# A long convolution ahead of adapters and a gated FFN: order of the first loads, smaller kernel groups, other engines for part of the elementwise work, TensorE in source order

## The chip, the cores and the metric

The kernel runs on one core of one Trainium2 chip, in float32. The metric is device microseconds of one execution, the median of three runs. Engine names are those of the profile: PE is TensorE (PEld its weight load), DVE VectorE, ACT ScalarE, POOL GpSimd, SP SyncE. ACTq and SPq are the instruction streams of ACT and SP where they issue DMAs.

## The reference

x has 32 sequences of 64 channels and 1024 steps. Four residual stages follow each other; the change concerns the first.

```python
# 0: S4D convolution along the 1024 steps, one kernel per channel h
dt = exp(log_dt); A = -exp(log_A_real) + 1j * A_imag; dtA = A * dt[:, None]
Ct = (C[..., 0] + 1j * C[..., 1]) * (exp(dtA) - 1.0) / A
K = 2.0 * einsum('hn,hnl->hl', Ct, exp(dtA[:, :, None] * arange(1024))).real   # 64 states n
y = irfft(rfft(x, n=2048) * rfft(K, n=2048))[..., :1024] + x * D[:, None]
x = x + y * (arange(1024) < length[:, None, None])
# 1, 2: a 1024x1024 weight per sequence, chosen by an index
x = x + einsum('bsi,boi->bso', x, weight1[ids1])
x = x + einsum('bij,bkj->bik', x, weight2[ids2])
# 3: gated FFN, 2752 hidden units, low-rank adapters of rank 16 by index
x = x + ffn(x)
```

## The kernel before

**Stages.** x is held transposed in four chunks of eight sequences (`xs[c]`, 2 MB each): positions within a block of 128 on the partitions; block, sequence and channel along the free side. `convolution` (from L533) does stage 0 for all chunks. Chunks 2 and 3 are then parked in DRAM. `adapters(0)` does stages 1 and 2 of chunk 0, and `ffn(c)` does stage 3 of chunk c with the adapters of chunk c + 1 woven in between. Adapter weights (`wa`, 512 KB a load, 512 loads) go through a pool of nine buffers.

**The order of work.** A scheduler places each instruction in its engine's stream by the order of the source and by when it expects the operands; each engine then runs its own stream strictly in that order and waits on semaphores. Tiles of a tag share a number of buffers, and a tile waits for its buffer to come free. `tc.manual_schedule(engines={PE})` takes TensorE's stream out of the scheduler's hands: its instructions run in the order of the source. Before, it covers only what follows the convolution (L525). `tc.issue_after(ins)` puts what it encloses behind `ins` in the same engine's stream, with no wait for `ins` to end.

**The first loads.** SP issues the constant table `cst` (L105), the ids (L110, L114), the state space parameters `par` (L552), the lengths `ln` (L554), and then the first three `uf`. ACT issues the four loads of x (L668) at the same time. From `par` VectorE works out exp, sine and cosine of small tiles (128x64), the discretised coefficients (L584 to L655) and the mask of the lengths (L662).

**The convolution kernels, `kernels(g)`.** A group is 16 heads (channels), four groups. The kernel of a head is 1024 numbers, written as 32x32: position l = 32a + b, so exp(dtA l) is a product of two factors. `powers` (L690) makes angles `theta` (`bth`) and logarithms of sizes `rho` (`brho`) for both factors by multiplying a column per head with a table along l: four VectorE multiplications of 128x512. `rho` goes through Exp on ACT; three sines (`sine`, L570: seven VectorE instructions each and one Sin on ACT), and five more products on VectorE give `gt` and `et`. TensorE multiplies them, a 32x32 product a head (`pk`, L721). VectorE copies the result out (`ks`, L729) and adds D in the first position (L731). ACT's queue stores it to DRAM in rows (`kp`, L734) behind a row of zeros (L733). The tiles of `kernels` have one buffer per tag, `gt`, `et`, `ks` two.

**The convolution proper, `convolve(g, kp)`.** For four heads at a time, `uf` (x of these heads in reversed order, 512 KB, L741) is loaded, and for each pair of heads `hk` (1 MB, L746): the Toeplitz matrix, read from `kp` with a step of one element from partition to partition. Both have three buffers. Eight matmuls of falling width a head accumulate into `pc` (L757), VectorE multiplies with the mask into `tmp` (two buffers, L764), and four VectorE additions, one for each chunk, add `tmp` to x (L775). The loop of L777 to L781 traces `kernels(g + 1)` before `convolve(g)`.

Of the kernel before, what the change touches and what calls it, by code (L numbers as in the profile page):

```python
# [32 lines left out]
NE = 16  # L33
NPIECE = 2 * BC
AT_GATED, AT_DOWN = 4, 5
HG = 16
LQ = 32
KROW = P + L

# [22 lines left out]
def kernel(  # L62
# [39 lines left out]
        return psum.tile([P, 512], F32, tag="acc", name=name, bufs=2)  # L102

    cst = cpool.tile([P, CO_N], F32, tag="cst", name="cst")
    nc.sync.dma_start(cst, consts)  # L105
    ident = cst[:, CO_ID : CO_ID + P]
    bmask = cst[:, CO_BM : CO_BM + TC]

    ids_sb = cpool.tile([1, 3 * B], I32, tag="ids", name="ids_sb")
    nc.sync.dma_start(ids_sb, ids)  # L110
# [9 lines left out]
    for c in range(NCK):  # L120
# [4 lines left out]
            None,  # L125
            ALU.add,
        )

    def x_tile(pool, c, tag):
        return pool.tile([P, KT, TC], F32, tag=tag, name=f"x{c}")

    xs = [x_tile(xpool, c, "x") for c in range(2)]
    parked = []
    with tc.tile_pool(name="x2pool", bufs=1) as x2pool:
        late = [x_tile(x2pool, c, f"x{c}") for c in range(2, NCK)]
        convolution(tc, cst, xt, xf, ssm, lens, xs + late, ps_tile)
        for c, x_c in enumerate(late, 2):
            d = dpool.tile([P, KT, TC], F32, tag=f"xd{c}", name=f"xd{c}")  # L140
            nc.scalar.dma_start(d, x_c)
            parked.append(d)

# [248 lines left out]
    def prepare(c):  # L392

        x_c = xs[c]
        for name, table in (("g", ag), ("u", au)):
            at = columns(table, c, KT, f"{name}_{c}")
            low_rank(at, KT, lambda i: (x_c[:, i, :], P), tms[name], f"{name}_{c}")
        xq = [
            x_c[:, k * KH : (k + 1) * KH, t * TH : (t + 1) * TH]
            for k in (0, 1)  # L400
            for t in (0, 1)
        ]

        xd = hpool.tile([P, 7, KH, TH], F32, tag="xd", name=f"xd_{c}")
        for i, q in enumerate((0, 2, 3)):
            nc.scalar.copy(xd[:, 4 + i], xq[q])
        xb = moving(*xq, *(xd[:, i] for i in range(4)))
        return (xd[:, 4], xd[:, 5], xd[:, 6], *xb[3:])
# [113 lines left out]
                    other(AT_DOWN)  # L522
        return ready

    with tc.manual_schedule(engines={PE}):  # L525
        for _ in adapters(0):
            pass
        xb = prepare(0)
        for c in range(NCK):
            xb = ffn(c, xb, adapters(c + 1) if c + 1 < NCK else iter(()))  # L530


def convolution(tc, cst, xt, xf, ssm, lens, xs, ps_tile):  # L533

# [8 lines left out]
    with ExitStack() as ctx:  # L543
# [6 lines left out]

        par = s1.tile([P, 6, H], F32, tag="par", name="par")
        nc.sync.dma_start(par, ssm)  # L552
        ln = s1.tile([P, B], I32, tag="len", name="ln")
        nc.sync.dma_start(ln, lens.partition_broadcast(P))  # L554
        aim, cre, cim, dskip = (par[:, i, :] for i in range(2, 6))
# [108 lines left out]
            )  # L664
        maskf = mask.rearrange("p k b -> p (k b)")

        for c in range(NCK):
            nc.scalar.dma_start(xs[c], xt[:, c])  # L668

        zero = s1.tile([HG, P], F32, tag="zero", name="zero")  # L670
        nc.vector.memset(zero, 0.0)

        def kernels(g):

            h0 = g * HG
            shape = [P, HG, LQ]

            def over_l(ap):
                return ap[:, h0 : h0 + HG].unsqueeze(2).to_broadcast(shape)

            def over_h(at):
                return cst[:, at : at + LQ].unsqueeze(1).to_broadcast(shape)

            n = [0]

            def big(tag):
                n[0] += 1
                return s1.tile(shape, F32, tag=f"b{tag}", name=f"b{tag}{g}_{n[0]}")

            def powers(at, tag):  # L690
                theta, rho = big(f"th{tag}"), big(f"rho{tag}")
                tt(theta, over_l(y), over_h(at), ALU.mult)
                tt(rho, over_l(x), over_h(at), ALU.mult)
                nc.scalar.activation(rho, rho, AF.Exp)
                return theta, rho

            th1, rho1 = powers(CO_LVAL, "1")
            th2, rho2 = powers(CO_LVAL + LQ, "2")

            def flat_sine(theta, i, tag):  # L700
# [10 lines left out]
            gt = s2.tile(shape, F32, tag="gt", name=f"gt{g}")  # L711
            et = s2.tile(shape, F32, tag="et", name=f"et{g}")
# [7 lines left out]
            for i in range(HG):  # L720
                nc.tensor.matmul(  # L721
                    ps[:LQ, i * LQ : (i + 1) * LQ],
                    gt[:, i, :],
                    et[:, i, :],
                    start=True,
                    stop=True,
                )
            ks = s2.tile([LQ, HG, LQ], F32, tag="ks", name=f"ks{g}")
            nc.vector.tensor_copy(ks.rearrange("a h b -> a (h b)"), ps[:LQ, : HG * LQ])  # L729
            k0 = ks[0:1, :, 0]  # L730
            tt(k0, k0, dskip[0:1, h0 : h0 + HG], ALU.add)  # L731
            kp = dram.tile([HG, KROW], F32, tag=f"kp{g}", name=f"kp{g}")
            nc.scalar.dma_start(kp[:, :P], zero)  # L733
            nc.scalar.dma_start(kp[:, P:].rearrange("h (a b) -> a h b", b=LQ), ks)  # L734
            return kp

        def convolve(g, kp):
            for h0 in range(0, HG, 4):
                ha = g * HG + h0
                uf = s3.tile([P, 4, KT, B], F32, tag="uf", name=f"uf{ha}")  # L740
                nc.sync.dma_start(uf, xf[:, ha : ha + 4])  # L741
                tmp = s2.tile([P, 4, KT * B], F32, tag="tmp", name=f"tmp{ha}")
                for i in range(0, 4, 2):
                    hk = s3.tile([P, 2, L], F32, tag="hk", name=f"hk{ha + i}")

                    nc.sync.dma_start(  # L746
                        hk,
                        bass.AP(
                            tensor=kp.tensor,
                            offset=kp[h0 + i : h0 + i + 1, 1:2].offset,  # L750
                            ap=[[1, P], [KROW, 2], [1, L]],
                        ),
                    )
                    ps = ps_tile(f"pc{ha + i}").rearrange("p (i t) -> p i t", i=2)
                    for j in range(2):
                        for d in range(KT):
                            nc.tensor.matmul(  # L757
                                ps[:, j, d * B :],
                                hk[:, j, d * P : (d + 1) * P],
                                uf[:, i + j, : KT - d, :].rearrange("p k b -> p (k b)"),  # L760
                                start=(d == 0),
                                stop=(d == KT - 1),
                            )
                    tt(  # L764
                        tmp[:, i : i + 2, :],
                        ps,
                        maskf.unsqueeze(1).to_broadcast([P, 2, KT * B]),
                        ALU.mult,
                    )
                tv = tmp.rearrange("p i (k b) -> p k b i", b=B)  # L770
                for c in range(NCK):
                    xv = xs[c].rearrange("p k (b h) -> p k b h", h=H)[
                        :, :, :, ha : ha + 4
                    ]
                    tt(xv, xv, tv[:, :, c * BC : (c + 1) * BC, :], ALU.add)  # L775

        ready = kernels(0)  # L777
        for g in range(H // HG):
            nxt = kernels(g + 1) if g + 1 < H // HG else None
            convolve(g, ready)  # L780
            ready = nxt  # L781


# [131 lines left out]
```

## Time and profile before

| what | value |
|---|---|
| time, median of 3 runs | 2580.82 us (2580.62 to 2581.64) |
| the profiled execution: time | 2580.24 us |
| the profiled execution: span | 2578.5 us |
| PE busy | 2483.8 us (96%) |
| DVE busy | 1061.7 us (41%) |
| ACT busy | 255.5 us (10%) |
| POOL busy | 45.8 us (2%) |
| first pk on PE | 40.4 us after the span's start |
| first pc on PE | 61.5 us |
| last mask multiplication (tmp) | 212.7 us |
| first adapter matmul (pa) | 214.1 us |

The span runs from the first to the last instruction of the profiled execution; the time counts what lies around it too. "Busy" counts an instruction's duration; idle time in the profile is put down to what ended it, the releaser. The chain of waits follows the work that ended last back through releasers; a stretch of it that belongs to PE cannot be shortened by another engine.

### The profile page before, as it was taken

The numbers are of one execution on the slowest core, as the hardware profiler recorded it, in microseconds if no ns is written. First come the engines' busy times: TensorE is split into PE (matmuls) and PEld (weight loads), VectorE is DVE, ScalarE is ACT, GpSimd is POOL, SyncE is SP. The second block draws the span as 40 slices with busy tenths as digits, with TensorE's granted clock in tenths as the row PEclk, the third lists the DMA queues.
The fourth block names the chain that finished last, engine by engine and source line by source line (L and its number), as shares of the span: only waits on it lengthen the run. The fifth ranks groups of instructions, "written<-read, shape, count | busy, mean of one in ns | idle before, by whom it ended". The sixth has DMA issues, their size and how long they took to land.

```text
span 2578.5 us, 33259 instructions
## 1 busy us (share of the span) xinstructions
PE 2483.8 (96%) x12896; PEld 1795.9 (70%) x12896; DVE 1061.7 (41%) x2174; ACT 255.5 (10%) x468; POOL 45.8 (2%) x52
## 2 busy tenths in 40 slices
PE   1998999999999999999999999999999999999999
PEld 0994225767676686667776686667766688888877
DVE  8632004343334353333334453343334354444444
ACT  3100001010001101110011100110010101100110
POOL 0000000000000000000000000000000000000000
PEclk9999999999999999999999999999999999999999
DMA  7787997464746447554746547555655443223212
GB/s 288 258 281 271 406 409 270 172 230 152 241 156 231 168 151 263 182 213 155 244 163 226 171 137 265 189 203 171 217 197 207 163 145 107 84 70 108 82 52 67
DMA packets 176160, 500.63 MB, mean 194 GB/s; under 512 B 19778, under 2 KB 69122, under 8 KB 174978
## 3 DMA queue, kind: packets, MB, share of 16 engines
q1 hardware_dynamic: 145762, 453.63, 50.0%
q10 hardware_dynamic: 26144, 31.24, 3.5%
q0 software_dynamic: 4096, 13.63, 1.8%
q8 instruction: 102, 1.67, 0.3%
q14 instruction: 56, 0.46, 0.1%
HBM read 485.56 MB, written 12.88 MB: 193 GB/s over the span
## 4 chain that ended last, share of the span: by engine, by line
PE 90%; DMA 7%; DVE 2%; ACT 0%; ACTq 0%; issue 0%; SPq 0%; DVEq 0%
PE pf L351 42%; PE po L480 21%; PE pa L182 14%; PE pc L757 6%; DMA wa<-in_w 5%; PE pf L298 4%; PE py L200 1%; PE pl_d L275 1%; PE po L298 1%; DMA x<-xd 1%; DMA out_y<-x 0%; DMA ln<-in_lens 0%; PE pl_g L275 0%; PE pl_u L275 0%; DMA raw_g<-in_ag 0%
## 5 line engine op out<-in xcount | busy, mean ns | idle before, releaser
L351 PE MATMUL pf<-xd,wf 128*128 128x256 f32 (+1 forms) x2816 | 677.9, 384 | 0.0
L351 PEld LDWEIGHTS pf<-xd,wf 128*128 128x128 f32 (+1 forms) x2816 | 517.8, 187 | 131.4 <-issue 58.8
L182 PE MATMUL pa<-wa,x 128*64 128x512 f32 x2048 | 494.1, 602 | 25.6 <-DMA wa<-in_w 20.6
L351 PE MATMUL pf<-xd,s 128*128 128x256 f32 (+1 forms) x2112 | 507.9, 383 | 2.2 <-DVE s L319 2.2
L351 PEld LDWEIGHTS pf<-xd,s 128*128 128x128 f32 (+1 forms) x2112 | 388.8, 187 | 86.7 <-issue 31.9
L182 PEld LDWEIGHTS pa<-wa,x 128*64 128x64 f32 x2048 | 149.3, 137 | 335.1 <-issue 250.4
L480 PE MATMUL po<-act,wd 128*128 128x256 f32 x704 | 177.0, 385 | 0.0
L480 PE MATMUL po<-actd,wd 128*128 128x256 f32 x704 | 172.9, 379 | 0.0
L480 PE MATMUL po<-actd,s 128*128 128x256 f32 x704 | 172.9, 379 | 0.0
L376 DVE TENSOR_TENSOR c<-pf,c 128x256 f32<-128x256 f32 (+1 forms) x88 | 37.3, 424 | 328.8 <-PE pf L351 328.8
L480 PEld LDWEIGHTS po<-act,wd 128*128 128x128 f32 x704 | 130.3, 190 | 33.3 <-issue 11.0
L757 PE MATMUL pc<-uf,hk 128*128 128x256 f32 (+7 forms) x1024 | 149.1, 309 | 0.0
L757 PEld LDWEIGHTS pc<-uf,hk 128*128 128x128 f32 x1024 | 145.2, 192 | 3.6
L480 PEld LDWEIGHTS po<-actd,s 128*128 128x128 f32 x704 | 133.6, 190 | 18.4
L480 PEld LDWEIGHTS po<-actd,wd 128*128 128x128 f32 x704 | 133.6, 190 | 18.4
L318 DVE TENSOR_TENSOR s<-wf 128x512 f32<-128x512 f32 x88 | 60.7, 689 | 143.3 <-DMA wf<-in_wu 65.9
L379 DVE TENSOR_TENSOR c<-pf,u 128x256 f32<-128x256 f32 (+1 forms) x88 | 37.3, 424 | 169.5 <-PE pf L298 169.5
L204 DVE TENSOR_TENSOR x<-py,x 128x512 f32<-128x512 f32 x64 | 41.3, 686 | 153.0 <-PE py L200 152.7
L381 DVE TENSOR_TENSOR c<-pf,u 128x256 f32<-128x256 f32 (+1 forms) x88 | 37.3, 424 | 132.4 <-PE pf L351 132.4
L318 DVE TENSOR_TENSOR s<-wd 128x384 f32<-128x384 f32 x64 | 33.4, 521 | 141.2 <-PE po L480 81.4
L192 ACT COPY y<-pa 128x512 f32<-128x512 f32 x64 | 37.5, 586 | 499.7 <-PE pa L182 475.1
L480 PE MATMUL po<-act,s 128*128 128x256 f32 (+1 forms) x352 | 86.5, 379 | 0.0
(147 smaller groups left out, 1574.0 us busy)
## 6 DMA issues: line engine op xcount, KB each, us to landing
wa<-in_w SPq DMA_DIRECT2D x512, 512.0 KB, 6.7
wf<-in_wg SPq DMA_DIRECT2D x88, 512.0 KB, 3.6
wf<-in_wu SPq DMA_DIRECT2D x88, 512.0 KB, 3.6
wd<-in_wd SPq DMA_DIRECT2D x96, 384.0 KB, 4.0
hk<-kp SPq DMA_DIRECT2D x32, 1024.0 KB, 7.4
x<-in_xt ACTq DMA_DIRECT2D x4, 2048.0 KB, 11.4
uf<-in_xf SPq DMA_DIRECT2D x16, 512.0 KB, 8.5
wd<-in_wd SPq DMA_DIRECT2D x32, 256.0 KB, 3.7
```

Source lines behind the costliest of these rows:

```text
L182: nc.tensor.matmul(acc[i][s * H : (s + 1) * H, :], xs[c][:, kt, lo + s * H : lo + (s + 1) * H], wts[s][:, i * 512 : (i + 1) * 512], start= ...
L192: nc.scalar.copy(y[:, i * 512 : (i + 1) * 512], acc[i])
L200: nc.tensor.transpose(ps[:, i, :], y[:, (q + i) * P : (q + i + 1) * P], ident)
L204: nc.vector.tensor_add(cols, ps, cols)
L298: nc.tensor.matmul(ps, b[rows_], t[rows_], start=start, stop=True, skip_group_check=True,)
L318: nc.vector.tensor_add(s1, a21, a22)
L351: nc.tensor.matmul(ps, ws[j][:, kt, :n], xb[j][:, kt, :], start=start and kt == 0, stop=kt == KH - 1, skip_group_check=True,)
L376: nc.vector.tensor_add(cq[:n, 3], pb, cq[:n, 3])
L379: nc.vector.tensor_add(cq[:n, 2], pc, u[:n])
L381: nc.vector.tensor_add(cq[:n, 1], pb, u[:n])
L480: nc.tensor.matmul(pss[j], ws[j][:k, i, :], ab[m - m0][j], start=(m == m0 and home[j] % 2 == 0), stop=(m == m1 - 1), skip_group_check=True,)
L757: nc.tensor.matmul(ps[:, j, d * B :], hk[:, j, d * P : (d + 1) * P], uf[:, i + j, : KT - d, :].rearrange("p k b -> p (k b)"), start=(d == ...
```

## The change

- `consts` is loaded inside `convolution`, after `par`; the loads of the ids and the four index instructions made from them are traced after the convolution.
- The four loads of x move from ahead of the groups to behind the store of the first group's kernels in ACT's stream.
- The groups are 8, 8, 12, 12, 12 and 12 heads instead of four of 16; tiles keep the size of the largest and are cut.
- The four multiplications of `powers` and the four additions to x go to GpSimd. ACT copies `pk` out instead of VectorE.
- `convolve` now does four heads; `kernels(g + 1)` is traced between the last but one and the last four heads of group g.
- `manual_schedule` covers the whole kernel, so TensorE's stream in the convolution is in the order of the source too.

```diff
-HG = 16
+GROUPS = (8, 8, 12, 12, 12, 12)
+HG = max(GROUPS)
...
     cst = cpool.tile([P, CO_N], F32, tag="cst", name="cst")
-    nc.sync.dma_start(cst, consts)
...
+    ctx.enter_context(tc.manual_schedule(engines={PE}))
+    with tc.tile_pool(name="x2pool", bufs=1) as x2pool:
+        late = [x_tile(x2pool, c, f"x{c}") for c in range(2, NCK)]
+        convolution(tc, cst, consts, xt, xf, ssm, lens, xs + late, ps_tile)
...
     ids_sb = cpool.tile([1, 3 * B], I32, tag="ids", name="ids_sb")
     nc.sync.dma_start(ids_sb, ids)
...
-    with tc.tile_pool(name="x2pool", bufs=1) as x2pool:
-        late = [x_tile(x2pool, c, f"x{c}") for c in range(2, NCK)]
-        convolution(tc, cst, xt, xf, ssm, lens, xs + late, ps_tile)
...
         nc.sync.dma_start(par, ssm)
+        nc.sync.dma_start(cst, consts)
         ln = s1.tile([P, B], I32, tag="len", name="ln")
...
-        for c in range(NCK):
-            nc.scalar.dma_start(xs[c], xt[:, c])
...
+        loaded = []
         def kernels(g):
-            h0 = g * HG
-            shape = [P, HG, LQ]
+            h0, hg = sum(GROUPS[:g]), GROUPS[g]
+            shape = [P, hg, LQ]
...
-                tt(theta, over_l(y), over_h(at), ALU.mult)
-                tt(rho, over_l(x), over_h(at), ALU.mult)
+                nc.gpsimd.tensor_tensor(theta, over_l(y), over_h(at), ALU.mult)
+                nc.gpsimd.tensor_tensor(rho, over_l(x), over_h(at), ALU.mult)
...
-            nc.vector.tensor_copy(ks.rearrange("a h b -> a (h b)"), ps[:LQ, : HG * LQ])
+            ks = s2.tile([LQ, HG, LQ], F32, tag="ks", name=f"ks{g}")[:, :hg]
+            nc.scalar.copy(ks.rearrange("a h b -> a (h b)"), ps[:LQ, : hg * LQ])
...
-            nc.scalar.dma_start(kp[:, :P], zero)
-            nc.scalar.dma_start(kp[:, P:].rearrange("h (a b) -> a h b", b=LQ), ks)
+            nc.scalar.dma_start(kp[:, :P], zero[:hg])
+            load = nc.scalar.dma_start(kp[:, P:].rearrange("h (a b) -> a h b", b=LQ), ks)
+            loaded.append(load.ins)
...
-        def convolve(g, kp):
-            for h0 in range(0, HG, 4):
+        def convolve(kp, row, ha):
...
-                    tt(xv, xv, tv[:, :, c * BC : (c + 1) * BC, :], ALU.add)
+                nc.gpsimd.tensor_tensor(xv, xv, tv[:, :, c * BC : (c + 1) * BC, :], ALU.add)
         ready = kernels(0)
-        for g in range(H // HG):
-            nxt = kernels(g + 1) if g + 1 < H // HG else None
-            convolve(g, ready)
+        for c in range(NCK):
+            with tc.issue_after(loaded[0]):
+                nc.scalar.dma_start(xs[c], xt[:, c])
+        ha = 0
+        for g, hg in enumerate(GROUPS):
+            nxt = None
+            for row in range(0, hg, 4):
+                convolve(ready, row, ha)
+                ha += 4
+                if row + 8 == hg and g + 1 < len(GROUPS):
+                    nxt = kernels(g + 1)
             ready = nxt
```

More of the change, by code (lines that the diff above doesn't have):

```diff
@@ L104, with x_tile @@
     cst = cpool.tile([P, CO_N], F32, tag="cst", name="cst")
-    nc.sync.dma_start(cst, consts)
     ident = cst[:, CO_ID : CO_ID + P]
     bmask = cst[:, CO_BM : CO_BM + TC]
+    def x_tile(pool, c, tag):
+        return pool.tile([P, KT, TC], F32, tag=tag, name=f"x{c}")
+    xs = [x_tile(xpool, c, "x") for c in range(2)]
+    parked = []
+    ctx.enter_context(tc.manual_schedule(engines={PE}))
+    with tc.tile_pool(name="x2pool", bufs=1) as x2pool:
+        late = [x_tile(x2pool, c, f"x{c}") for c in range(2, NCK)]
+        convolution(tc, cst, consts, xt, xf, ssm, lens, xs + late, ps_tile)
+        for c, x_c in enumerate(late, 2):
+            d = dpool.tile([P, KT, TC], F32, tag=f"xd{c}", name=f"xd{c}")
+            nc.scalar.dma_start(d, x_c)
+            parked.append(d)
     ids_sb = cpool.tile([1, 3 * B], I32, tag="ids", name="ids_sb")
@@ L127 @@
         )
[L131 to L135, printed above, removed]
-    with tc.tile_pool(name="x2pool", bufs=1) as x2pool:
-        late = [x_tile(x2pool, c, f"x{c}") for c in range(2, NCK)]
-        convolution(tc, cst, xt, xf, ssm, lens, xs + late, ps_tile)
[L139 to L142, printed above, removed]
     loads = []
@@ L523, in ffn, with convolution @@
         return ready
[L525 to L528, printed above, removed]
-        for c in range(NCK):
-            xb = ffn(c, xb, adapters(c + 1) if c + 1 < NCK else iter(()))
-def convolution(tc, cst, xt, xf, ssm, lens, xs, ps_tile):
+    for _ in adapters(0):
+        pass
+    xb = prepare(0)
+    for c in range(NCK):
+        xb = ffn(c, xb, adapters(c + 1) if c + 1 < NCK else iter(()))
+def convolution(tc, cst, consts, xt, xf, ssm, lens, xs, ps_tile):
     nc = tc.nc
@@ L665, in convolution @@
         maskf = mask.rearrange("p k b -> p (k b)")
-        for c in range(NCK):
-            nc.scalar.dma_start(xs[c], xt[:, c])
         zero = s1.tile([HG, P], F32, tag="zero", name="zero")
         nc.vector.memset(zero, 0.0)
+        loaded = []
         def kernels(g):
-            h0 = g * HG
-            shape = [P, HG, LQ]
+            h0, hg = sum(GROUPS[:g]), GROUPS[g]
+            shape = [P, hg, LQ]
             def over_l(ap):
-                return ap[:, h0 : h0 + HG].unsqueeze(2).to_broadcast(shape)
+                return ap[:, h0 : h0 + hg].unsqueeze(2).to_broadcast(shape)
             def over_h(at):
@@ L684, in kernels, with big @@
             n = [0]
-            def big(tag):
+            def big(tag, pool=s1):
                 n[0] += 1
-                return s1.tile(shape, F32, tag=f"b{tag}", name=f"b{tag}{g}_{n[0]}")
+                return pool.tile([P, HG, LQ], F32, tag=f"b{tag}", name=f"b{tag}{g}_{n[0]}")[
+                    :, :hg
+                ]
             def powers(at, tag):
                 theta, rho = big(f"th{tag}"), big(f"rho{tag}")
-                tt(theta, over_l(y), over_h(at), ALU.mult)
-                tt(rho, over_l(x), over_h(at), ALU.mult)
+                nc.gpsimd.tensor_tensor(theta, over_l(y), over_h(at), ALU.mult)
+                nc.gpsimd.tensor_tensor(rho, over_l(x), over_h(at), ALU.mult)
                 nc.scalar.activation(rho, rho, AF.Exp)
@@ L710, in kernels @@
             p2 = flat_sine(th2, 0, "e")
-            gt = s2.tile(shape, F32, tag="gt", name=f"gt{g}")
-            et = s2.tile(shape, F32, tag="et", name=f"et{g}")
+            gt, et = big("gt", s2), big("et", s2)
             tt(et, p2, rho2, ALU.mult)
@@ L719, in kernels @@
             ps = ps_tile(f"pk{g}")
-            for i in range(HG):
+            for i in range(hg):
                 nc.tensor.matmul(
@@ L727, in kernels @@
                 )
-            ks = s2.tile([LQ, HG, LQ], F32, tag="ks", name=f"ks{g}")
-            nc.vector.tensor_copy(ks.rearrange("a h b -> a (h b)"), ps[:LQ, : HG * LQ])
+            ks = s2.tile([LQ, HG, LQ], F32, tag="ks", name=f"ks{g}")[:, :hg]
+            nc.scalar.copy(ks.rearrange("a h b -> a (h b)"), ps[:LQ, : hg * LQ])
             k0 = ks[0:1, :, 0]
-            tt(k0, k0, dskip[0:1, h0 : h0 + HG], ALU.add)
-            kp = dram.tile([HG, KROW], F32, tag=f"kp{g}", name=f"kp{g}")
@@ L733, in kernels @@
-            nc.scalar.dma_start(kp[:, :P], zero)
-            nc.scalar.dma_start(kp[:, P:].rearrange("h (a b) -> a h b", b=LQ), ks)
-            return kp
-        def convolve(g, kp):
-            for h0 in range(0, HG, 4):
[L739 to L774, printed above, removed]
-                    tt(xv, xv, tv[:, :, c * BC : (c + 1) * BC, :], ALU.add)
@@ L777, in convolution @@
-        ready = kernels(0)
-        for g in range(H // HG):
-            nxt = kernels(g + 1) if g + 1 < H // HG else None
-            convolve(g, ready)
+            tt(k0, k0, dskip[0:1, h0 : h0 + hg], ALU.add)
+            kp = dram.tile([hg, KROW], F32, tag=f"kp{g}", name=f"kp{g}")
+            nc.scalar.dma_start(kp[:, :P], zero[:hg])
+            load = nc.scalar.dma_start(kp[:, P:].rearrange("h (a b) -> a h b", b=LQ), ks)
+            loaded.append(load.ins)
+            return kp
+        def convolve(kp, row, ha):
+            uf = s3.tile([P, 4, KT, B], F32, tag="uf", name=f"uf{ha}")
+            nc.sync.dma_start(uf, xf[:, ha : ha + 4])
+            tmp = s2.tile([P, 4, KT * B], F32, tag="tmp", name=f"tmp{ha}")
+            for i in range(0, 4, 2):
+                hk = s3.tile([P, 2, L], F32, tag="hk", name=f"hk{ha + i}")
+                nc.sync.dma_start(
+                    hk,
+                    bass.AP(
+                        tensor=kp.tensor,
+                        offset=kp[row + i : row + i + 1, 1:2].offset,
+                        ap=[[1, P], [KROW, 2], [1, L]],
+                    ),
+                )
+                ps = ps_tile(f"pc{ha + i}").rearrange("p (i t) -> p i t", i=2)
+                for j in range(2):
+                    for d in range(KT):
+                        nc.tensor.matmul(
+                            ps[:, j, d * B :],
+                            hk[:, j, d * P : (d + 1) * P],
+                            uf[:, i + j, : KT - d, :].rearrange("p k b -> p (k b)"),
+                            start=(d == 0),
+                            stop=(d == KT - 1),
+                        )
+                tt(
+                    tmp[:, i : i + 2, :],
+                    ps,
+                    maskf.unsqueeze(1).to_broadcast([P, 2, KT * B]),
+                    ALU.mult,
+                )
+            tv = tmp.rearrange("p i (k b) -> p k b i", b=B)
+            for c in range(NCK):
+                xv = xs[c].rearrange("p k (b h) -> p k b h", h=H)[:, :, :, ha : ha + 4]
+                nc.gpsimd.tensor_tensor(xv, xv, tv[:, :, c * BC : (c + 1) * BC, :], ALU.add)
@@ L781, in convolution @@
+        ready = kernels(0)
+        for c in range(NCK):
+            with tc.issue_after(loaded[0]):
[8 more added lines that the diff above has]
+                    nxt = kernels(g + 1)
             ready = nxt
```

## The prediction

> **What bounds the kernel now.** I read the slices of the span first, then the chain of waits in order of time, then the timeline around its first TensorE work, then stretches and DMA issues.
>
> ```profile
> PE   1998999999999999999999999999999999999999
> DMA  7787997464746447554746547555655443223212
> ```
>
> A digit stands for a fortieth of the span (64 us). TensorE is idle in the first slice alone; after it only removing TensorE work, or the DMA limit near 250 to 400 us (1.03 busy, 409 GB/s), could bring anything. The change touches none of that.
>
> ```profile
> 2.62 9.38 DMA ln<-in_lens
> ...
> 59.63 1.92 PE pk L721 x32
> 61.55 38.23 PE pc L757 x256
> 99.78 1.13 PE pk L721 x32
> 100.90 36.91 PE pc L757 x256
> 137.82 1.13 PE pk L721 x32
> 138.95 73.73 PE pc L757 x512
> 212.70 0.70 DVE tmp L567
> 213.42 0.60 DVE x L567
> 214.06 7.14 PE pa L182 x32
> ...
> 224.38 15.88 DMA wa<-in_w
> ```
>
> Start, length, what: 12 us of waiting for tables, VectorE until 59.63, then TensorE without a gap to 212.70. The adapter weights that follow (wa) wait for TensorE to free their buffers, so that whatever moves 212.70 moves the end one for one.
>
> ```profile
> 40.41 1.91 PE L721 MATMUL pk<-et,gt 128*32 128x32 f32 x32 [40.41 <-DVE gt L567]
> ...
> 44.16 0.33 ACTq L734 DMA_DIRECT2D kp<-ks  x1
> ...
> 45.92 1.42 SPq L746 DMA_DIRECT2D hk<-kp  x3
> ```
>
> ```profile
> 59.63 1.92 PE L721 MATMUL pk<-et,gt 128*32 128x32 f32 x32 [17.30 <-DVE et L567]
> ```
>
> Group 0's kernels are made at 40.4 and its first three hk are asked for at 46, but TensorE's order puts group 1's pk first, and it sits 17.3 us for VectorE. That, the wait for tables and the size of group 0 are what can be won.
>
> ```profile
> 40.00:60.00 20.00, 2.28 (x39) 2.15 (x40) 19.69 (x39) 8.64 (x10) 0.00 (x0) 1.00 0.49 173
> 60.00:80.00 20.00, 20.00 (x148) 19.33 (x146) 18.42 (x36) 7.98 (x10) 0.00 (x0) 1.00 0.49 157
> 100.00:200.00 100.00, 100.00 (x740) 97.66 (x737) 40.69 (x71) 0.00 (x0) 0.00 (x0) 1.00 0.82 278
> ```
>
> Columns: busy PE, PEld, DVE, ACT, POOL, clock, DMA share, GB/s. VectorE is full to 80 us; DMA is at 0.82 while TensorE convolves, so 8 MB more there is not free.
>
> ```profile
> hk<-kp SPq DMA_DIRECT2D x32, 1024.0 KB, 7.4
> x<-in_xt ACTq DMA_DIRECT2D x4, 2048.0 KB, 11.4
> uf<-in_xf SPq DMA_DIRECT2D x16, 512.0 KB, 8.5
> ...
> kp<-ks ACTq DMA_DIRECT2D x4, 64.0 KB, 1.7
> ```
>
> The tile views add: hk lands in 5.4 to 10.3 us, kp in 1.7 to 5.8.
>
> [...] a zero row stored behind the last x on ACT's queue took 4.5 us for 8 KB. [...] the first pk took 1.92 us against 1.13, and the first hk 6.0 against 4.6.
>
> **The change part by part.**
>
> *Tables first.* par was issued at 2.0 and landed in 7.9 us beside x. Now first and alone, it should need about 2.3 us (estimate between kp's 1.7 for 64 KB and wf's 3.6 for 512), so VectorE starts at 3.2 instead of 9.7. cst follows before ln; the wait for ln (1.05 us) stays or halves.
>
> *Eight heads, powers on GpSimd.* From 9.7 to the end of gt at 40.4 VectorE works 30.7 us. Kernel 0 in it, by start-to-start steps: four powers of 0.60, three sines of 0.40+0.35+3x0.60+0.40+0.34 = 3.3, five products of 0.60: 15.3. With 256 elements instead of 512 (lines through the 64- and 512-element steps: 0.34 for two inputs, 0.23 and 0.20 for one) and no powers: 7.3. Group 1's share in this stretch falls from 2.5 to 0.4. The four powers are now GpSimd's: [...] I take 3. So 30.7 - 8.0 - 2.1 + 3 = 23.6, and gt is ready at 26.8 (24 to 29).
>
> *First hk.* pk to kp issue was 3.75 us; half a pk (-1.0) and a smaller copy (-0.25) make 2.5: kp at 29.3, landed 31.3, hk asked for. The x loads start at 29.7, on ACT's queue right behind. From 12 to 24 us SP's queue got 2.94 MB and ACT's 2.18 side by side, so hk gets 57% of 420 GB/s: the first lands at 37.7. TensorE starts 22 us earlier than 59.6.
>
> *x now collides with the convolution.* Before it was hidden in the first 38 us. kp1's store comes behind all four x loads in ACT's queue. Until it can move, DMA has x (8.4 MB), hk0 to hk3 (4.2) and uf3 (0.5): 13.1 MB at 420 GB/s, 31.2 us, to 60.9. Then kp1 1.7 and hk4 5.4: 68.0. TensorE, with two groups of four heads, the cold start and pk1, is out of work at 37.7 + 18.4 + 1.4 + 0.6 = 58.1: a 10 us wait that wasn't there. If kp1 is not held, it is 3 us.
>
> *What follows.* 56 heads at 147.5/64 = 2.305 us each (the 148.9 us of pc without the cold start): 129.1; pk for 48 heads at 1.13/16: 3.4; warming up again 1.4. So 68.0 + 133.9 = 201.9 without further waits.
>
> *Kernels four heads ahead.* In source order pk of the next group stands ahead of the last four heads, which cover 9.2 us. Before, a group of 16 heads (37 us) covered it. From pk's end: copy on ACT, the addition of D, issue: 1.6 (1.84 before, with larger tiles); kp 3.0 (1.7 free, 5.8 worst; one uf is in flight); hk 5.4; with 0.1 to issue it is 10.1. So 0.9 late, and 0.3 for standing behind activations or VectorE instructions in order: 1.2 each at four more borders, 4.8. Bounds 0 and 5.7 (kp 5.8, hk 7.4). End of the convolution: 206.7 against 212.7.
>
> *Additions on GpSimd.* 64 of 256 elements: [...] 0.54 before on VectorE. A group of 12 heads is 27.7 us of TensorE; in it VectorE has 10.2 of kernel and 3.6 of masks [...] The last addition is longer: +0.4 us before the adapters. Copies of pk on ACT (0.4 us) lie beside TensorE in its idle time; the ids and their indices, now late in the text, aren't needed before 214.
>
> *Sum.* -6.0 + 0.4 = -5.6 us from the profiled execution (2580.24, of which the span is 2578.5), 2574.6; the median is 0.6 above it, so 2575.
>
> **The rivals.**
> - *The handoff is the bound (slower).* Every group's kernels go TensorE, ACT, VectorE, ACT's queue, DRAM, SP's queue with 9.2 us of cover. For it: 5.8 us for kp and 7.4 for hk are in this trace, both under the load that the convolution makes. Against: at a border no other hk can be in flight, as the slots wait. It decides from 2.6 us a border on ((212.7 - 201.9 - 0.4) / 4); at 5.7 the sum is +12: 2593.
> [...]
> - *Neither x nor the handoff is felt.* TensorE starts at 36 and has 152.9 us, the cold start in it, with 3 us for sharing DMA and 1 more of warming: 193, or -19: 2561.5. For it: DMA has 18% free, and three hk of buffer.
> - *Nothing moves,* since x and the borders eat just what the start wins: that is the forecast's upper part, to 2580.
>
> **How the numbers follow.** Forecast 0.46, with a range of its own of 2569 to 2581; neither felt 0.25; handoff 0.19[...]. A measurement of this kernel tells 0.2% (5.2 us) from nothing; the forecast lies near that line, so its chance goes 0.24 faster, 0.20 same, 0.02 slower. With 0.25 faster, 0.19 slower, [...]: 0.49, 0.23, 0.28. Range 2561 to 2593: the two outer cases' values.
>
> **What would show it.** First pc at 36 to 39 us; then TensorE idle about 10 us near 58 with kp1 landing behind x; later holes of 0 to 3 us ahead of the first pc of each group, ended by DMA hk; the mask of the last head near 207. GpSimd's x at 0.6 to 0.9 us. I am wrong if pc starts after 42, if TensorE waits for gt or et after its start [...], or if kp1 lands within 6 us of issue.

## The result, and the profile after

The changed kernel takes 2599.91 us (median of 4 runs, 2596.60 to 2602.91); the kernel before took 2580.84 us in the same session. The ratio is 1.0073, with an interval of 1.0056 to 1.0090: slower by 0.7%, where 2575.0 had been predicted, and above the range. The profiled execution took 2601.19 us, its span is 2599.4 us.

The timeline of TensorE in the changed kernel, from the span's start to the first adapter matmul: start, length, what runs, and in brackets the idle time ahead of it with what ended it.

```profile
29.83 1.06 PE L722 MATMUL pk<-bet,bgt 128*32 128x32 f32 x16 [29.83 <-DVE bet L568]
52.56 7.67 PE L758 MATMUL pc<-uf,hk 128*128 128x256 f32 x32 [21.67 <-DMA hk<-kp]
62.10 4.79 PE L758 MATMUL pc<-uf,hk 128*128 128x256 f32 x32 [1.87 <-DMA hk<-kp]
68.00 0.69 PE L722 MATMUL pk<-bet,bgt 128*32 128x32 f32 x16 [1.11 <-DVE bet L568]
68.62 9.39 PE L758 MATMUL pc<-uf,hk 128*128 128x256 f32 x64
80.84 9.36 PE L758 MATMUL pc<-uf,hk 128*128 128x256 f32 x64 [2.83 <-ACT brho L696]
90.12 0.94 PE L722 MATMUL pk<-bet,bgt 128*32 128x32 f32 x24
91.00 9.38 PE L758 MATMUL pc<-uf,hk 128*128 128x256 f32 x64
107.23 21.43 PE L758 MATMUL pc<-uf,hk 128*128 128x256 f32 x128 [6.84 <-DVE bsp L568]
...
140.53 18.56 PE L758 MATMUL pc<-uf,hk 128*128 128x256 f32 x128 [1.69 <-DMA hk<-kp]
...
171.32 20.14 PE L758 MATMUL pc<-uf,hk 128*128 128x256 f32 x128 [2.04 <-DMA hk<-kp]
...
203.26 27.76 PE L758 MATMUL pc<-uf,hk 128*128 128x256 f32 x192 [1.62 <-DMA hk<-kp]
232.71 7.51 PE L183 MATMUL pa<-wa,x 128*64 128x512 f32 x33 [1.69 <-POOL x L774]
```

Group 0's pk is at 29.8 instead of 40.4, but the first pc comes only at 52.6, 9.0 us ahead of before's 61.55. From there to the first pa it takes 180.15 us where before took 152.5 (61.55 to 214.06), so the adapters begin 18.65 us later, which is most of the loss. The extra 27.6 us are holes, idle times of TensorE (1.87 + 1.11 + 2.83 + 6.84 + 1.69 + 2.04 + 1.62 = 18.0), slower pc (the pc lines, those left out too, sum to 156.63 against 149.06 in the same view of before: 7.6, of which 2.9 behind the hole of 6.84 and 1.6 behind that of 2.04, at a granted clock of 0.50 and 0.56 there, and 1.7 in the first 32, which took 7.67 us against 6.0 before) and pk, now inside this stretch (2.1); the pieces of these views overlap by some tenths.

The first of these places, in the chain of waits of the changed kernel (start, length, what):

```profile
33.45 1.53 DMA kp<-ks
35.50 26.55 DMA hk<-kp
62.10 4.80 PE pc L758 x32
```

The kernels of group 0 are in DRAM at 35; from then until 62 the chain is one DMA wait, for the second hk. The first was asked for at 35.06 and TensorE started on it at 52.56, 17.5 us later. Each hk of 1 MB landed in 7.4 us on the median before, and the tile view of hk after has the same median with a longest of 26.5 us. What the DMA engines did meanwhile is in the DMA view of the changed kernel from 45 to 55 us (queue: packets, MB, share of the 16 engines' time; q10 is ACT's queue, with x alone, q1 is SP's, with hk):

```profile
q10 hardware_dynamic: 227, 3.21, 77.9%
q1 hardware_dynamic: 227, 0.86, 22.2%
```

The engines are full (100.1% for the two together), and each queue moved exactly as many packets as the other, 227. But a packet of x is 14.1 KB on the mean (3.21 MB / 227), one of hk 3.8 KB, so that hk's queue got 21% of the bytes.

The trace of the kernel before held this number too. Its DMA view from 14 to 18 us, while x was in flight beside wa and uf on SP's queue:

```profile
q10 hardware_dynamic: 84, 1.38, 80.2%
q1 hardware_dynamic: 88, 0.35, 21.2%
```

Again nearly equal counts of packets, 84 and 88, and SP's queue has 20% of the bytes. The prediction read 12 to 24 us in one piece and got 57% for SP. From 12 to 13 us ACT's queue moved nothing at all, and from 20 to 24 us it moved 0.08 MB of x: the mean was over time in which there was nothing to share.

The second place is the holes of 2.83 and 6.84 us, ahead of the first pc of groups 1 and 2. The releasers in their brackets, an Exp and a product, don't feed pc. By SP's timeline the hk they need were asked for at 74.53 and 100.87 and landed 6.3 and 6.4 us later, so what came late is the store of the kernels. VectorE beside GpSimd in the changed kernel, timeline around the end of the first group:

```profile
67.53 0.41 DVE L568 TENSOR_TENSOR bet<-bse,brho 128x256 f32<-128x256 f32 x1
67.69 3.22 POOL L774 TENSOR_TENSOR x<-x,tmp 128x256 f32<-128x256 f32 x3 [26.57 <-DVE tmp L568]
67.86 1.22 DVE L576 SCALAR_TENSOR_TENSOR bre<-bk,bth 128x384 f32<-128x384 f32 x1
...
69.11 1.09 DVE L577 SCALAR_TENSOR_TENSOR bre<-bk,bre 128x384 f32<-128x384 f32 x1
70.24 1.09 DVE L578 SCALAR_TENSOR_TENSOR bre<-bk,bre 128x384 f32<-128x384 f32 x1
70.88 1.14 POOL L695 TENSOR_TENSOR brho<-sm,cst 128x384 f32<-128x384 f32 x1
71.36 0.87 DVE L579 TENSOR_SCALAR bre<-bre,cst 128x384 f32<-128x384 f32 x1
71.98 0.94 POOL L694 TENSOR_TENSOR bth<-sm,cst 128x384 f32<-128x384 f32 x1
72.05 0.52 ACT L696 ACTIVATE brho<-brho 128x384 f32<-128x384 f32 x1 [2.97 <-POOL brho L695]
...
72.16 0.79 DVE L568 TENSOR_TENSOR ks<-ks,par 1x8 f32<-1x8 f32 x1
...
74.90 0.55 DVE L576 SCALAR_TENSOR_TENSOR brp<-bk,bth 128x384 f32<-128x384 f32 x1
```

A VectorE instruction of this kind with 384 elements takes 0.55 us with GpSimd idle (at 74.90) and 1.09 to 1.22 beside it. The addition of D, eight numbers that group 1's store waits for, stands in order behind four slowed instructions. It takes 0.79 us itself and ends with GpSimd's multiplication (72.95 and 72.92); without GpSimd's work it takes 0.15 (e3, below). ACT's Exp waits for GpSimd's brho, and where the copy of pk stands behind that Exp, it waits too: group 2's pk ended at 91.06, its copy started at 94.75 (a table load of 1.28 us and a Sin stand between as well), D at 98.38, the store was issued at 99.21. In the prediction this part took 1.6 us; here it took 8.15, and the hole is 6.84.

### The profile page after: what moved, and what is told of

It is laid out like the page before. It is cut to its first block, busy times and chain, and to the rows that moved or that the text cites. A ratio compares the mean times of both kernels' runs of the same rounds, so it can differ in the third digit from the quotient of the medians.

```text
span 2599.4 us, 33379 instructions
## 1 busy us (share of the span) xinstructions
PE 2493.2 (96%) x12896; PEld 1804.3 (69%) x12896; DVE 1046.3 (40%) x2144; ACT 264.9 (10%) x488; POOL 126.7 (5%) x140
## 3 DMA queue, kind: packets, MB, share of 16 engines
q1 hardware_dynamic: 145762, 453.63, 49.1%
## 4 chain that ended last, share of the span: by engine, by line
PE 85%; DMA 9%; DVE 4%; issue 1%; ACTq 1%; ACT 0%; POOL 0%; SPq 0%; DVEq 0%; POOLq 0%
PE pf L352 42%; PE po L481 20%; PE pa L183 14%; DMA wa<-in_w 5%; PE pf L299 4%; PE pc L758 2%; DMA hk<-kp 2%; PE py L201 1%; PE pl_d L276 1%; DMA x<-xd 1%; PE po L299 1%; DMA kp<-ks 0%; DMA out_y<-x 0%; DVE bk L574 0%; ACTq L251 0%
## 5 line engine op out<-in xcount | busy, mean ns | idle before, releaser
L758 PE MATMUL pc<-uf,hk 128*128 128x256 f32 (+7 forms) x1024 | 156.6, 316 | 38.6 <-DMA hk<-kp 28.9
L758 PEld LDWEIGHTS pc<-uf,hk 128*128 128x128 f32 x1024 | 151.2, 198 | 43.6 <-DMA hk<-kp 23.8
L226 POOL DMA_INDIRECT bgu<-in_bgu,rows x44 | 41.7, 949 | 1951.7 <-PE pf L299 1951.2
```

The costliest lines, as they stand in the source:

```text
L226: nc.gpsimd.indirect_dma_start(out=t, out_offset=None, in_=table, in_offset=bass.IndirectOffsetOnAxis(ap=rows[:, c, piece : piece + 1], axis=0
L758: nc.tensor.matmul(ps[:, j, d * B :], hk[:, j, d * P : (d + 1) * P], uf[:, i + j, : KT - d, :].rearrange("p k b -> p (k b)"), start=(d == ...
```

## The experiments

Each short diff is against the changed kernel unless another is named. Ratios are against the kernel before, with intervals. A border is the passage from one group to the next, where the kernels are handed to the convolution through DRAM.

| run | what it is | us | ratio | first pc, us |
|---|---|---|---|---|
| after | the change | 2599.91 | 1.0073 [1.0056, 1.0090] | 52.6 |
| e1_x_early | x loaded early | 2587.56 | 1.0031 [1.0019, 1.0042] | 49.5 |
| e2_small_packets | x in 4 KB packets | 2594.02 | 1.0050 [1.0033, 1.0067] | 46.0 |
| e3_vectore | nothing on GpSimd | 2592.80 | 1.0047 [1.0030, 1.0064] | 51.8 |
| e4_both | e1 and e3 | 2581.02 | 1.0002 [0.9993, 1.0011] | 49.2 |
| e5_wa_late | e4, first wa later | 2582.07 | 1.0003 [0.9994, 1.0011] | 39.2 |
| e6_pk_earlier | e4, kernels eight heads ahead | 2575.94 | 0.9982 [0.9975, 0.9989] | 49.1 |
| e7_all | e5 and e6 | 2565.86 | 0.9941 [0.9924, 0.9958] | 38.1 |
| e8_groups_only | only groups and source order | 2581.96 | 1.0007 [0.9998, 1.0016] | 48.5 |
| e9_adds_pool | e7, additions on GpSimd | 2570.88 | 0.9965 [0.9953, 0.9978] | 38.0 |
| e10_powers_pool | e7, angles on GpSimd | 2568.36 | 0.9958 [0.9941, 0.9974] | 38.9 |
| e11_x_late | e7, x behind the first store | 2584.60 | 1.0017 [1.0010, 1.0024] | 50.7 |

### x loaded early (e1)

My theory after the first reading was that x beside hk cost most (called X below), the rival that GpSimd's work did, beside which VectorE's instructions had taken 1.09 to 1.22 us instead of 0.55 (L).

```diff
+        tanh = nc.scalar.activation(t, x, AF.Tanh, scale=0.5)
+        for c in range(NCK):
+            with tc.issue_after(tanh.ins):
+                nc.scalar.dma_start(xs[c], xt[:, c])
...
-        for c in range(NCK):
-            with tc.issue_after(loaded[0]):
-                nc.scalar.dma_start(xs[c], xt[:, c])
```

> The changed kernel with the four loads of x behind the tanh in ACT's stream (about 8.5 us) instead of behind the store of group 0's kernels. Theory X (x's long packets starve hk, which sets the first convolution): the first hk lands about 6 us after it is asked for instead of 17.5, pc starts near 41 us instead of 52.6, the two holes before 68 us go, the end of the convolution moves from 231 to 213 to 219, time 2580 to 2588. Theory L [...]: pc starts earlier but VectorE is late all the same, time within 4 us of the changed kernel's 2600. Theory H (the handoff through DRAM): between the two, as the holes before the first pc of each group stay at 2 to 7 us.

2587.56 us, 12.3 less than the changed kernel: the time is where X put it. But the first pc comes at 49.5, not near 41. ACT's timeline in this run shows why:

```profile
14.66 13.24 ACTq L670 DMA_DIRECT2D x<-in_xt  x3
27.93 1.28 ACT L700 ACT_TABLE_LOAD   x1 [13.02 <-DMA wa<-in_w]
...
36.47 0.35 ACTq L739 DMA_DIRECT2D kp<-ks  x1
```

ACT stood 13 us over the issue of x; what ended this, by the profile, was the landing of a load of wa, on SP's queue. The Exp of the first kernels waited behind it (pk at 34.3 instead of 29.8), and the store kp then followed x in ACT's queue: hk was asked for at 43.26, 6.8 us after the store was issued. So the start gives only 3.1 us of e1's gain. The rest lies behind it: the two holes around 61 and 67 are gone and the early groups' holes are smaller (0.21 and 4.96).

### x in small packets (e2)

```diff
-                nc.scalar.dma_start(xs[c], xt[:, c])
+            for q in range(0, KT, 2):
+                with tc.issue_after(loaded[0]):
+                    nc.scalar.dma_start(xs[c][:, q : q + 2], xt[:, c, q : q + 2])
```

> The changed kernel with each load of x cut into four of 4 KB a partition, at the same place. [...] hk (4 KB packets) gets half of the bandwidth beside x instead of a fifth: the first hk lands 7 to 9 us after it is asked for, pc starts at 42 to 44 us; the store of group 1's kernels still stands behind x in ACT's queue, so a new hole near 65 us of about 8 us takes part of it back, time 2592 to 2597. [...] hk lands 15 us or more after it is asked for and the time stays within 3 us of 2600.

The first forecast is for the case that the size of the packets sets the shares, the last for the case that it doesn't. x stays where the change put it; its packets shrink, and there are sixteen issues instead of four. The DMA view of this run, 40 to 45 us:

```profile
q1 hardware_dynamic: 213, 0.85, 51.2%
q10 hardware_dynamic: 217, 0.77, 44.9%
```

Still nearly as many packets from either queue (213 and 217), but now 52% of the bytes are hk's, and the first hk lands 10.6 us after it was asked for (35.37 to 46) instead of 17.5 (35.06 to 52.56). The counts of packets stay even, and the bytes went with the packets' size (4.0 and 3.5 KB on the mean). The hk is still slower than the 7 to 9 us that were expected; the two queues together moved 324 GB/s here and 408 in the window of the changed kernel. The time falls by 5.9 us, less than the 6.6 us of the first pc: a hole of 6.45 us opens ahead of the second pk. ACT's timeline has its cause, which the expectation lacked:

```profile
34.14 29.66 ACTq L781 DMA_DIRECT2D x<-in_xt  x16
63.85 0.42 ACT L582 ACTIVATE bse<-bre 128x256 f32<-128x256 f32 x1 [30.17 <-DMA x<-in_xt]
```

ACT stood 29.7 us over the sixteen issues, with a Sin of group 1's kernels behind them.

### Nothing on GpSimd (e3), and both (e4)

```diff
-                nc.gpsimd.tensor_tensor(theta, over_l(y), over_h(at), ALU.mult)
-                nc.gpsimd.tensor_tensor(rho, over_l(x), over_h(at), ALU.mult)
+                tt(theta, over_l(y), over_h(at), ALU.mult)
+                tt(rho, over_l(x), over_h(at), ALU.mult)
...
-                nc.gpsimd.tensor_tensor(xv, xv, tv[:, :, c * BC : (c + 1) * BC, :], ALU.add)
+                tt(xv, xv, tv[:, :, c * BC : (c + 1) * BC, :], ALU.add)
```

> The changed kernel with the angles and the additions to x back on VectorE. Theory X: pc starts within 2 us of 52.6, time no more than 5 us below 2600. Theory L: no instruction of VectorE takes over 0.75 us, the additions 0.6; gt and et come 2 to 3 us earlier, the hole of 6.8 us ahead of group 2 shrinks to 2, time 2586 to 2592.

> Both: x behind the tanh and the angles and additions on VectorE. If X and L add up: the sum of the gains of the two single edits, 2570 to 2578, below the kernel before. If L is only felt because x made TensorE late (VectorE's stream stands behind masks that wait for TensorE), the gains don't add: within 3 us of the edit of x alone.

e3 gains 7.1 us, a time between the two forecasts, and e4 18.9: nearly the sum of 12.3 and 7.1, so the costs of x's place and of GpSimd add up. In e3 the first pc hardly moves (51.8) and pk only by 0.4, so GpSimd was not what made the start late; the hole of 2.83 us is gone and that of 6.84 falls to 1.68. The two holes ahead of them grow, to 3.03 and 2.75, as VectorE now does the additions too: the 7.1 us is a net gain. The addition of D for group 1, in VectorE's timeline of e3:

```profile
72.52 0.15 DVE L568 TENSOR_TENSOR ks<-ks,par 1x8 f32<-1x8 f32 x1
```
e4 was expected at 2570 to 2578 and missed. It starts 12.4 us ahead of before (49.18 against 61.55) and is no faster: ACT still stands 14.6 us over x until wa has landed, kp is issued at 35.12 and hk asked for at 43.05, and four borders cost 1.79, 2.00, 1.55 and 1.92 us.

### The first adapter weights later (e5), kernels earlier (e6), both (e7)

The first nine loads of wa are put behind a load of hk in the middle of the convolution in SP's stream (`hks` collects the loads of hk); `kernels(g + 1)` is traced after the first four heads of a group, so that eight heads cover it in the groups of twelve.

```diff
-    loads = []
+    loads = [hks[16]] * 2
...
-                if row + 8 == hg and g + 1 < len(GROUPS):
+                if row == 0 and g + 1 < len(GROUPS):
```

> x behind the tanh, angles and additions on VectorE, and the first nine loads of adapter weights (4.7 MB) put behind an hk load in the middle of the convolution in SP's stream, so that they no longer share DMA with x. Theory X says that in the run with both edits x still was in the way: ACT stood 14.6 us with a load of x that waited for wa to land, and the store of group 0's kernels lay 8 us behind x in ACT's queue. Then pk moves from 33.0 to 29 to 30 us, the store lands in 2 us, pc starts at 37 to 40 us instead of 49.2, time 2569 to 2573. If it was not x and wa that held the store and pk, pc stays at 47 to 50 and the time at 2579 to 2583.

> x behind the tanh, angles and additions on VectorE, and the kernels of the next group traced behind the first four heads of a group, so that in groups of 12 eight heads of TensorE work cover the handoff through DRAM instead of four. Theory H: the holes of 1.5 to 2.0 us ahead of the first pc of groups 3, 4 and 5 go, that ahead of group 2 stays (its predecessor has 8 heads), time 5 to 6 us less than with both edits alone: 2575 to 2576.5. If instead VectorE is not done with gt and et by then, TensorE waits ahead of pk, and the time stays at 2580 or rises.

> All of it: x behind the tanh, wa late, angles and additions on VectorE, kernels of the next group behind the first four heads. If the three terms are separate, the gains add: about 2581 - 10 - 5 = 2566 (2562 to 2570), 0.5% below the kernel before. If TensorE, started 10 us earlier, catches up with VectorE, holes ahead of pk eat part of it: 2570 to 2576.

e5 does at the start what was expected and more (pk 25.8, first pc 39.2), but it missed its 2569 to 2573 us and gains nothing on e4: later borders grow to 4.58 and 5.18 us, with slower pc behind them (21.48 us for 128 against 18.56 behind the first). SP's timeline in e5 at that border:

```profile
135.05 0.89 SPq L177 DMA_DIRECT2D wa<-in_w  x2
141.36 2.24 SPq L751 DMA_DIRECT2D hk<-kp  x3
```

kp was issued at 136.04, one microsecond after 1 MB of wa, and hk could be asked for only 5.3 us later. e6 gains 5.1 us on e4: the holes of the later groups are gone, those of 1.31 and 1.80 stay. With twice the cover the borders behind the moved wa show no hole either, and e7 gets both. TensorE's timeline in e7:

```profile
26.22 1.06 PE L726 MATMUL pk<-bet,bgt 128*32 128x32 f32 x16 [26.22 <-DVE bgt L568]
38.12 11.24 PE L763 MATMUL pc<-uf,hk 128*128 128x256 f32 x64 [10.85 <-DMA hk<-kp]
49.30 0.69 PE L726 MATMUL pk<-bet,bgt 128*32 128x32 f32 x16
49.92 9.38 PE L763 MATMUL pc<-uf,hk 128*128 128x256 f32 x64
59.63 9.36 PE L763 MATMUL pc<-uf,hk 128*128 128x256 f32 x64 [0.33 <-DMA hk<-kp]
...
81.01 9.36 PE L763 MATMUL pc<-uf,hk 128*128 128x256 f32 x64 [1.83 <-DVE brp L579]
...
148.35 46.19 PE L763 MATMUL pc<-uf,hk 128*128 128x256 f32 x320
195.94 7.94 PE L183 MATMUL pa<-wa,x 128*64 128x512 f32 x34 [1.40 <-DVE x L568]
```

Two holes of 2.2 us together are left, pa starts 18.1 us ahead of before, and e7 at 2565.86 us beats both kernels: 0.9941 [0.9924, 0.9958].

### Groups and source order alone (e8)

Loads in their old order, everything on VectorE, the copy of pk too (the other lines of the change undone).

> The other half of the change alone: six smaller groups and TensorE in source order, but tables, x and ids loaded as in the kernel before, and angles, additions and the copy of pk on VectorE. Theory X: x is out of the way by about 40 us as before, pk comes near 33 us, pc at 41 to 46, and with holes of 1 to 2 us at four or five borders the time is 2570 to 2577: faster than before. If the smaller groups and the source order are themselves what costs (handoff), the time is 2581 or more.

2581.96 us, no different from before: theory X missed, and the second expectation, that small groups and source order cost what they win, came true. The first pc is 13 us earlier (48.5), later than expected, as the first group's store was issued only 5.5 us after its pk, with stores of zero rows and Exps ahead of it in ACT's stream. Still pa starts at 213.9 against 214.1. Between lie five borders of 1.20, 2.12, 1.51, 1.39 and 1.36 us, 3.8 us of slower pc (11.30 for 9.2 and 20.21 for 18.56) and the pk of six groups, which before stood in part ahead of the first pc. Small groups bring the start forward and pay it back at the borders. Group size and source order were not taken apart, nor were the tables' place and ACT's copy of pk tried alone.

### One part put back into the best kernel (e9, e10, e11)

e9 has only the additions on GpSimd, e10 only the angles, e11 x behind the first store; their lines are those shown above, the other way round.

> The fastest kernel so far (x behind the tanh, wa late, kernels of the next group behind the first four heads, all on VectorE: 2565.9) with the additions to x back on GpSimd. Theory L for the additions: each takes 0.83 us undisturbed and over 1 beside the kernels' work, and doubles what VectorE does beside it; the holes of the first two groups' borders grow by 3 to 6 us, time 2570 to 2573. If only the angles cost, the time stays at 2566 to 2567 (0.4 us for the longer last addition).

> The fastest kernel so far with the angles (24 multiplications) on GpSimd. [...] pk0 0 to 1 us later: time 2566 to 2569. [...] 2570 or more, and the additions' run shows none.

> The fastest kernel so far with the loads of x back behind the store of group 0's kernels, nothing else. Theory X: DMA first moves x, pc starts at 48 to 52 us instead of 38.1, then the same holes: time 2576 to 2580. If x's place only mattered together with wa, GpSimd or the late handoff, within 3 us of 2566.

The 2570 or more of e10's expectation was for the case that GpSimd's whole cost lay in the angles. The additions cost 5.0 us. The angles cost 2.5 by the medians, but e10's runs spread over 7.3 us and its interval overlaps e7's, so this isn't clear of noise. Together they make 7.5, and taking both away in e3 had given 7.1. TensorE's timeline shows in e9 a hole of 3.21 us at the second border (1.83 in e7) and in e10 holes of 1.62 and 2.72. x put back costs 18.7 us, more than the 12.3 of e1 and more than was expected: the first pc is 12.6 us later (50.74 against 38.12), as expected, but holes of 2.21 and 2.76 us follow around 60 and 68, for which the expected time left no room, with slower pc behind them (20.24 us for 128, against 18.56). Of the 12.6 us, 2.2 are pk's (28.41 against 26.22): with x late, the scheduler orders ACT's and VectorE's streams differently.

## Why the prediction was wrong

**The step that failed first: the sharing of DMA.** "From 12 to 24 us SP's queue got 2.94 MB and ACT's 2.18 side by side, so hk gets 57% of 420 GB/s: the first lands at 37.7." It landed at 52.6. hk got 21% of the bytes in the window of 45 to 55 us, as SP's queue had got 20% at 14 to 18 us of the kernel before; with x in packets of 3.5 KB it got 52% (e2). hk was asked for at 35.1 instead of 31.3, most of which is pk's 3 us, and from asking to landing 17.5 us passed where the prediction had 6.4. In e7, where x has landed before, hk takes 6.3 us and the first pc starts at 38.1; that this is near the predicted number is no proof of the 57%, as nothing of x shares with hk there. That the mean of 12 us would hold for hk was the author's estimate.

**The hole near 58.** The second hk landed at 62.1, when x was about through, as predicted (60.9). That kp1 would be held behind x was the author's estimate, and it never was: TensorE started 15 us late, pk1 with it, and its store was issued only at 72.98 and landed within 1.6 us. The wait for hk4 that the prediction put here, 10 us, is the hole of 2.83 at 80.84; with those ahead of the second hk and of pk1 (1.87 and 1.11), which the sum lacked, it makes 5.8. The price of x was paid ahead of the first pc, not behind it. Two of the prediction's own signs of being wrong came true here: pc after 42, and kp1 landing within 6 us of issue.

**The border term, 1.2 us for each of four borders, was too small.** The four holes from 107.23 on sum to 12.2 us (6.84 + 1.69 + 2.04 + 1.62) against 4.8. The last three, undisturbed by the start, are 0.4 to 0.8 us over the estimate and inside its bounds of 0 and 5.7. The first, like that of 2.83, comes with VectorE slowed beside GpSimd, 1.09 to 1.22 us for 0.55. The prediction had given 0.10 of its weight (0.03 same, 0.07 slower) to VectorE held up by GpSimd; this was the author's estimate, and nothing in the trace of before showed it. What the sum missed is that it matters by the place in the stream, not by the total. It set the work of both engines against a whole group's 27.7 us of TensorE, while the store of the next group waits for a few instructions within it: VectorE's addition of D and ACT's copy, each behind slowed ones. e3 puts GpSimd's work as a whole at 7 us, and e9 the additions at 5.

**Warming up**, the prediction's name for slower pc after an idle time, was taken at 2.8 us (twice the 1.4 by which before's first 32 pc were slower, 6.0 against 4.6); pc took 156.6 us against the 147.5 without it, so it was 9.1. The first 32 pc are 3.1 of it (7.67 against 4.6, with a granted clock of 1.00 in the record), and 4.5 come behind the holes of 6.84 and 2.04, where the granted clock was 0.50 and 0.56.

These terms, counted from the first pc to the last mask, are -4.2 + 7.4 + 6.3 = +9.5 us, and with the 14.9 us by which the first pc was late they make 24.4: the convolution ended at 231.1 instead of 206.7.

**What held.** The end moves one for one with the convolution, apart from 2.3 us (after the first pa the changed kernel's profiled execution has 2366.7 us of span left, before's 2364.4); its runs spread over 6.3 us, and where these 2.3 come from I leave open. In the experiments' profiled executions this rest lies between 2364.4 and 2368.3, so that e7, 18.1 us ahead at the first pa, ends 14.4 ahead. GpSimd's addition was put at 0.6 to 0.9 us, the author's estimate, which no trace had shown; its median from 130 us on, in the view of its line, is 0.847 (0.828 to 1.255). The longer last addition was put at 0.4 us: the idle time ahead of the first pa is 1.69 us, and 1.40 before. With the tables first, VectorE starts on par at 3.20 us, as predicted (3.2). pk came at 29.8, 3 us behind the predicted 26.8, in which GpSimd's multiplications had 3 us, the author's estimate; without GpSimd's work pk is at 29.4 (e3). Most of the 3 us is the order of the streams: e11, which differs from e7 by x's place alone, has pk 2.2 us later, and in both it and the changed kernel ACT does the next group's Exp, with two table loads, ahead of group 0's last Sin (at 26.65 in the changed kernel, 23.59 in e7). e7's 26.2 shows that the operations themselves fit into the predicted time.

**The rivals.** The handoff is real: e6 takes 5.1 us from it, and e8 shows the borders eating a start 13 us earlier. It wasn't the bound, as without GpSimd and with x early it gives 1.5 to 2 us a border (e4), and the rival needed 2.6. What GpSimd costs is real too, at 7 (e3) of the 25 us. "Neither felt" (2561.5) is within 5 us of e7, a kernel in which x, GpSimd and the borders are dealt with; the change had them all against it.

## What to carry to other kernels

Before a large load is moved beside a stream of small transfers, count packets and bytes of the two queues in a window in which both are really in flight: here, with 227 packets each, the queue with packets of 14.1 KB had 79% of the bytes, with packets of 3.5 KB in e2 48%, and the first hk landed in 17.5, 10.6 and, with x out of the way in e7, 6.3 us. A pipeline in smaller pieces is worth only what its handoffs leave: follow the last small instruction of the handoff (here eight additions and a copy) in its engine's stream, and count what stands ahead of it, with the slow-down by a neighbour engine (0.55 to 1.09 and 1.22 us here). If several costs have the same place to show, take them away together once: e4, and e5 and e6 on top of it, looked like little or nothing, and e7 is 15.2 us faster than before.

## What the runs showed of the hardware

- In three windows in which two DMA queues were both in flight they moved about as many packets: 227 and 227 after (45 to 55 us, 14.1 KB against 3.8 KB, 3.21 MB against 0.86), 84 and 88 before (14 to 18 us, 1.38 MB against 0.35), 217 and 213 in e2 (40 to 45 us, 3.5 KB against 4.0, 0.77 MB against 0.85).
- ACT was held while it issued DMAs. It stood 13.0 us in e1 and 14.6 in e4 over loads of x, ended by the landing of wa as the profile has it, while SP took 15.6 and 14.6 us to issue its nine loads of wa. In e5, where wa comes later, three loads of x were issued in 1.4 us and pk is 7 us earlier than in e4. In e2 ACT stood 29.7 us over sixteen small loads of x. What exactly an issue waits for isn't shown.
- Beside GpSimd's additions VectorE's instruction with two inputs took 1.09 and 1.22 us instead of 0.55 in the changed kernel, and GpSimd's own addition went from 0.83 up to 1.63. An addition of eight numbers, 0.15 us in e3, took 0.79 and ended within 0.03 us of GpSimd's instruction. The multiplication with the mask, which reads PSUM, stayed at 0.68 to 0.69 us.
- Behind two of its holes TensorE's granted clock was lower in the changed kernel. With the hole of 6.84 us it was 0.50 from 103 to 113 us, and pc took 2.9 us more (21.43 for 18.56); behind that of 2.04 it was 0.56 from 171.3 to 175, and pc took 1.6 more (20.14); behind those of 1.69 and 2.83 it was 1.00, and pc took 18.56 for 128 and 9.36 for 64. In e3 pc took 1.65 us more behind a hole of 1.72 (20.21), in e4 no more behind one of 2.00 (18.56). The length of the hole alone doesn't order these, and what else does isn't shown.
